# A software-pipelined attention period in another order: scores in two halves, keys multiplied by their norms one period later

## The chip, the cores and the metric

The kernel runs on one core of one Trainium2 chip. The time is the device time of one execution in microseconds (us); lower is better. Each core has five engines that run side by side, each through its own instruction stream, strictly in the order written, and that wait for each other on semaphores: PE (TensorE, the matrix engine), DVE (VectorE), ACT (ScalarE), POOL (GpSimd) and SP (SyncE, which here issues most of the transfers). Matrix products land in PSUM, eight banks of 128 x 512 float32; DVE and ACT read them there.

## The reference

The program is a stack of four layers over 4 sequences of 512 tokens and 128 features: cross attention and a feed-forward part in each. The change touches only the feed-forward part of layer 2, which is itself a six-deep local transformer. One of its layers, cut to what matters:

```python
def attn_layer(x, Wqkv, qs, ksc, Wo):            # HEADS = 16, DIM_HEAD = 64, WINDOW = 32
    q, k, v = jnp.split(x @ Wqkv, 3, -1)         # split into heads
    q = l2norm(q) * qs
    k = l2norm(k) * ksc
    q = q * cos * scale + rotate_half(q) * sin * scale
    k = k * cos * inv + rotate_half(k) * sin * inv
    out = local_attention(q, k, v)               # a window of 32 sees itself and the one before
    return out @ Wo
...
sim = jnp.einsum('bhwie,bhwje->bhwij', bq, bk2) * QK_SCALE      # QK_SCALE = 8
sim = jnp.where(mask, -jnp.finfo(sim.dtype).max, sim)
attn = jax.nn.softmax(sim, -1)
out = jnp.einsum('bhwij,bhwje->bhwie', attn, bv2)
```

A gated feed-forward layer (layer norm, `W1` with a gelu gate, `W2`) follows each attention layer. Both are added to the stream.

## The kernel before

Everything around the local transformer is left as it is. `local_transformer` works on tiles of 128 tokens: 4 tiles make a sequence (a "row" in the code), 4 sequences a layer, 6 layers, so 96 tiles. The stream of a sequence is kept transposed in `Y[b]`. The order of the work is written out by hand; no planner moves it, and each engine runs its share in just that order.

The loop is a software pipeline. In period n it works on three tiles at once: tile n (`T`) goes from `Y` to rotated, normalised queries, keys and values; tile n-1 (`T1`) from there to exponentials of its scores; tile n-2 (`T2`) from there to the residual. The feed-forward layer of a finished sequence is cut into four phases and laid into the periods by `ff_stage`, at two places in each (`second` False or True).

The stages, with the lines of the profile:

- `queries_or_keys(T, kind, c)`: half c of the queries (kind 0) or keys (kind 1). One 128 x 512 product on PE (L1842) into one of two `mm` banks, and its squares on ACT (L1844).
- `rotate`: on DVE two products with the rotary tables (L1852, L1855) and the sum of the squares (L1864); on POOL the sum of the two products (L1865).
- `normalise`: on POOL and ACT the inverse norms of all 32 heads (L1875 to L1881, ACT's logarithm and exponential among them), then four POOL products of 128 x 512 (L1884), queries first, then keys.
- `turned`: two groups of four PE transposes (L621) into two `tr` banks, and an ACT copy of each (L1896), to `qT` or `kT`; for keys, POOL also puts the last 32 columns of the tile before at the head of `kT` (L1892, or zeros, L1894).
- `values(T, x0)`: one 128 x 512 product (L1919) into a `tr` bank, an ACT copy (L1920), and small transfers issued by SP that shift the windows (L1922 to L1930).
- `scores`: on PE 8 mask products (L1940) and then 64 products of 64 x 32 by 64 x 64 (L1949), into the two banks `sc`. The profile counts a float32 product as two matmuls and two weight loads, so 128 and 128.
- `softmax`: DVE takes the largest of each row (L1959) and subtracts it (L1960), ACT takes the exponential (L1965).
- `probabilities`: eight transposes (L621, `P`) and two ACT copies (L1970). `average(T, g)`: 32 small products (L1980) into the banks `av`. `normalised(T, g)`: a reciprocal and a product on DVE (L1989, L1990) that free `av`. `attended`: eight transposes (L621, `attn`) and two ACT copies (L1999). `project_out`: 8 products (L2004). `residual`: two DVE additions into `Y` (L2011).
- The feed-forward pieces use the same two banks `sc`: `ff_moments` (L2017 and DVE's statistics), `ff_norm` (L559, DVE), `ff_turn` (L2028), `ff_gate` (L2039), `ff_up` (L2050), `ff_down` (L2062).

On PE one period before is therefore: first query product, `P` transposes, second query product, a feed-forward piece, first averages, query transposes, first key product, second averages, key transposes, second key product, `attn` transposes, all scores, output product, two value products, a feed-forward piece.

Of the kernel before, what the change touches and what calls it, by code (L numbers as in the profile page):

```python
# [21 lines left out]
F32 = mybir.dt.float32  # L22
# [4 lines left out]
ALU = mybir.AluOpType  # L27
# [3 lines left out]
NT = S // 128  # L31
# [241 lines left out]
def tile_kernel(ctx: ExitStack, tc: tile.TileContext, A: dict, out: bass.AP):  # L273
# [1530 lines left out]
    def local_transformer(Y, lf, lw, columns, tabs):  # L1804

        with ExitStack() as es:
# [21 lines left out]
            class Tile:  # L1828


                def __init__(self, i, b, tt):
                    self.i, self.b, self.tt = i, b, tt
                    self.rot, self.raw, self.ss = {}, {}, None

# [32 lines left out]

            def normalise(T):


                n = 2 * LH
                ss = T.ss.rearrange("p a b -> p (a b)")
                y = small.tile([128, n], F32, name="rn_y")
                t = small.tile([128, n], F32, name="rn_t")
                G.tensor_scalar(ss, ss, 1e-24, -0.5, ALU.max, ALU.mult)  # L1875
                SC.activation(y, ss, AF.Ln, scale=-2.0)  # L1876
                SC.activation(y, y, AF.Exp, scale=-0.5)
                G.tensor_tensor(t, y, y, ALU.mult)
                G.tensor_tensor(t, t, ss, ALU.mult)
                G.tensor_scalar(t, t, 1.5, None, ALU.add)  # L1880
                G.tensor_tensor(y, y, t, ALU.mult)  # L1881
                for (kind, c), a in sorted(T.rot.items()):
                    o = LH * kind + 8 * c
                    G.tensor_tensor(a, a, bc(y[:, o : o + 8], [128, 8, LD], 2), ALU.mult)  # L1884

            def turned(T, kind):


                lead = 32 * kind
                t = qp.tile([128, LH // 2, lead + 128], F32, name="kT" if kind else "qT")  # L1890
                if kind and T.tt:
                    G.tensor_copy(t[:, :, 0:32], T.before.kT[:, :, 128:160])  # L1892
                elif kind:
                    G.memset(t[:, :, 0:32], 0.0)  # L1894
                for c in range(2):
# [3 lines left out]
                    )  # L1899
                if kind:  # L1900
                    T.kT = t
                else:
                    T.qT = t

# [26 lines left out]

            def scores(T):

                T.banks = pair("sc").rearrange("p z (k d) -> p z k d", d=64)
                for w in range(4):
                    for z in range(2):
                        r = slice(64 * (z ^ (w // 2)), 64 * (z ^ (w // 2)) + 64)
                        PE.matmul(  # L1940
                            T.banks[32 * w : 32 * w + 32, z], identb[r, r.start : r.start + 32],
                            maskw[r, int(w + T.tt == 0)], start=True, stop=False,
                            skip_group_check=True,
                        )
                for k in range(LH // 2):
                    for w in range(4):
# [7 lines left out]

            def softmax(T):

                P = tp.tile([128, LH // 2, 2, LD], F32, name="P", bufs=1)
                mx = small.tile([128, 2, LH // 2], F32, name="la_mx")
                V.tensor_reduce(mx, T.banks, AX.X, ALU.max)  # L1959
                V.tensor_tensor(  # L1960
                    P.rearrange("p k z d -> p z k d"), T.banks,
                    bc(mx, [128, 2, LH // 2, LD], 3), ALU.subtract,
                )
                T.P = P.rearrange("p k z d -> p k (z d)")
                SC.activation(T.P, T.P, AF.Exp, scale=8.0)  # L1965
# [55 lines left out]

            def ff_norm(F):
                layernorm(F.xn, F.xn, F.found)

# [48 lines left out]

            def ff_stage(F, phase, second):
                F.w1, F.w2 = loaded[F.i][2:]
                if phase == 0 and not second:
                    ff_moments(F)
                elif phase == 1:
                    ff_gate(F, 0, 1) if second else ff_turn(F)
                elif phase == 2 and second:  # L2080
                    ff_up(F, 0, 1)
                elif phase == 2:
                    ff_gate(F, 2)
                    SC.preload_act_table_set(EXP_LN)
                elif phase == 3:
                    ff_down(F) if second else ff_up(F, 2)

            tiles = [Tile(i, b, tt) for i in range(DEPTH) for b in range(B) for tt in range(NT)]  # L2090
# [3 lines left out]
            SC.preload_act_table_set(EXP_LN)  # L2094
            for n in range(len(tiles) + 2):
                T = tiles[n] if n < len(tiles) else None
                T1 = tiles[n - 1] if 0 <= n - 1 < len(tiles) else None
                T2 = tiles[n - 2] if 0 <= n - 2 < len(tiles) else None
                m, phase = divmod(n - 6, 4)
                F = rows[m] if 0 <= m < len(rows) else None  # L2100
                if T:
# [12 lines left out]
                    T.tabs = tabs[T.i]  # L2114
                    queries_or_keys(T, 0, 0)
                if T2:
                    probabilities(T2)
                if T:
                    queries_or_keys(T, 0, 1)
                    rotate(T, 0, 0)  # L2120
                if F:
                    ff_stage(F, phase, False)
                if T2:
                    average(T2, 0)
                if T1:
                    turned(T1, 0)
                if T:
                    queries_or_keys(T, 1, 0)
                if T2:
                    normalised(T2, 0)  # L2130
                if T:
                    rotate(T, 0, 1)
                if T2:
                    average(T2, 1)
                if T1:
                    turned(T1, 1)
                if T:
                    queries_or_keys(T, 1, 1)
                if T2:
                    normalised(T2, 1)  # L2140
                if T:
                    rotate(T, 1, 0)
                if T2:
                    attended(T2)
                if T and T.tt == NT - 1 and n + 1 < len(tiles):
                    swap(tiles[n + 1].b)
                if T1:
                    scores(T1)
                if T:
                    rotate(T, 1, 1)  # L2150
                if T:
                    normalise(T)
                if T1:
                    softmax(T1)
                if T2:
                    project_out(T2)
                    residual(T2)
                if F and phase == 0:
                    ff_norm(F)
                if T:  # L2160
                    values(T, 0)
                    values(T, 1)
                if F:
                    ff_stage(F, phase, True)
            return loaded[DEPTH - 1][2:]
# [133 lines left out]
```

## Time and profile before

| | |
|---|---|
| median of 3 runs | 2462.42 us (2460.44 to 2462.8) |
| the profiled execution | 2456.04 us |
| its span in the profile | 2454.2 us |
| first to last mask product of the local transformer (L1940) | 536.7 to 2152.8 us |
| PE busy | 2228.0 us (91%) |
| DVE, POOL, ACT busy | 1759.3, 1338.6, 1298.1 us (72%, 55%, 53%) |
| mean TensorE clock granted | 0.953 of full speed |

How to read what follows. A row of the timeline has the start in us from the beginning of the span, the time in us, the engine, the line, the operation, the tile written and read, the shapes, and how many instructions of that kind follow each other. In brackets stands how long the engine was idle before the row and what ended it. "issue" means that it waited for nothing that the profile shows. PEld is the loading of weights into the matrix engine, which overlaps its products. A busy PE is not PE at its peak, because the ends of matmuls are modelled; the time from the start of one block of rows to the start of the next says more.

### The profile page before, as it was taken

Reading aid. Unit: us, or ns where it says so; the run is one execution under the profiler, and the core shown is the slowest. Engines: PE = TensorE matmul, PEld = TensorE weight load, DVE = VectorE, ACT = ScalarE, POOL = GpSimd, SP = SyncE. Lnnn points to the kernel's source line nnn. Section 1 sums busy time; section 2 is a strip of 40 time slices with the busy share of each in tenths; the row PEclk is TensorE's granted clock in tenths of the full one; section 3 lists DMA queues with packets and bytes.
Section 4 is the critical chain, followed back from the end, with each engine's and each line's share of the span. In section 5 each row is a group of like instructions: output and inputs, shape, how many; then the busy total and the mean of one; then the engine's idle time right before and its main releaser. Section 6 shows DMA issues by size and latency. Waiting matters only on the chain. (4 is left out here: it accounts for less than half of the span.)

```text
span 2454.2 us, 86703 instructions
## 1 busy us (share of the span) xinstructions
PE 2228.0 (91%) x37341; PEld 1479.5 (60%) x37341; DVE 1759.3 (72%) x3896; ACT 1298.1 (53%) x2389; POOL 1338.6 (55%) x1862
## 2 busy tenths in 40 slices
PE   7958969978999999999999999999999999989676
PEld 3536734546666666666666666666666666644355
DVE  5545356866888888777887888887878788767422
ACT  3423325645666655666666666565666666525222
POOL 2141330256667676766667766766667666710433
PEclk9868989988999999999999999999999999989688
DMA  7201110016211121111211121111211111120023
GB/s 182 68 21 41 40 60 2 1 41 135 80 35 29 35 70 36 33 29 35 75 31 36 29 79 33 29 35 27 80 31 31 35 29 35 27 67 23 26 67 95
DMA packets 134298, 116.14 MB, mean 47 GB/s; under 512 B 29506, under 2 KB 102701, under 8 KB 133917
## 3 DMA queue, kind: packets, MB, share of 16 engines
q1 hardware_dynamic: 122037, 99.67, 15.8%
q0 software_dynamic: 4608, 7.35, 0.9%
q8 instruction: 296, 4.85, 0.9%
q10 hardware_dynamic: 7271, 3.58, 0.5%
q14 instruction: 86, 0.70, 0.1%
HBM read 42.84 MB, written 21.52 MB: 26 GB/s over the span
## 5 line engine op out<-in xcount | busy, mean ns | idle before, releaser
L1865 POOL TENSOR_TENSOR rc<-rc,rs 128x512 f32<-128x512 f32 x384 | 489.8, 1276 | 400.7 <-DVE rs L1855 326.3
L1842 PE MATMUL ps_mm<-wqk,y 128*128 128x512 f32 x768 | 397.2, 599 | 5.3 <-issue 3.5
L1884 POOL TENSOR_TENSOR rc<-rc,rn_y 128x512 f32<-128x512 f32 x384 | 388.6, 1044 | 7.5
L1852 DVE TENSOR_TENSOR rc<-ps_mm,tabs 128x512 f32<-128x512 f32 x384 | 262.5, 684 | 129.8 <-ACT sq L1844 126.5
L1844 ACT ACTIVATE sq<-ps_mm 128x512 f32<-128x512 f32 x384 | 231.2, 602 | 161.4 <-PE ps_mm L1842 108.0
L1855 DVE TENSOR_TENSOR rs<-ps_mm,tabs 128x512 f32<-128x512 f32 x384 | 261.5, 681 | 0.2 <-POOL rc L1865 0.2
L1864 DVE TENSOR_REDUCE ss<-sq 128x8 f32<-128x512 f32 x384 | 259.5, 676 | 0.0
L621 PE MATMUL ps_tr<-cst,rc 128*128 128x128 f32 x1536 | 210.9, 280 | 4.3 <-POOL rc L1884 4.0
L1980 PEld LDWEIGHTS ps_av<-v,PT 64*32 64x32 f32 x12288 | 138.1, 105 | 126.5 <-PE ps_tr L621 54.1
L2004 PE MATMUL ps_av<-aT,wo 128*128 128x128 f32 x1536 | 200.7, 283 | 2.4 <-issue 2.4
L2004 PEld LDWEIGHTS ps_av<-aT,wo 128*128 128x128 f32 x1536 | 181.0, 193 | 12.6 <-issue 3.9
L621 PEld LDWEIGHTS ps_tr<-cst,rc 128*128 128x128 f32 x1536 | 165.6, 142 | 24.4 <-POOL rc L1884 5.1
L1949 PE MATMUL ps_sc<-kT,qT 64*32 64x64 f32 x12288 | 148.1, 225 | 33.6 <-issue 32.9
L1980 PE MATMUL ps_av<-v,PT 64*32 64x65 f32 x12288 | 170.3, 225 | 6.2 <-DVE attn L1990 1.7
L1949 PEld LDWEIGHTS ps_sc<-kT,qT 64*32 64x32 f32 x12288 | 141.2, 105 | 44.2 <-issue 38.1
L1056 POOL DMA_INDIRECT back<-ye,to x80 | 78.8, 985 | 147.5 <-DVE ye L1170 104.0
L1842 PEld LDWEIGHTS ps_mm<-wqk,y 128*128 128x128 f32 x768 | 124.5, 192 | 56.3 <-issue 50.1
L1965 ACT ACTIVATE P<-P 128x1024 f32<-128x1024 f32 x96 | 101.4, 1057 | 97.3 <-DVE P L1960 97.3
L1876 ACT ACTIVATE rn_y<-ss 128x32 f32<-128x32 f32 x96 | 22.0, 229 | 237.9 <-POOL ss L1875 237.9
L802 ACT ACTIVATE P<-ps,deltaT 77x512 f32<-77x512 f32 x192 | 115.8, 683 | 56.7 <-PE ps L796 53.0
L1896 ACT COPY qT<-ps_tr 128x512 f32<-128x512 f32 x192 | 103.3, 589 | 74.6 <-PE ps_tr L621 74.3
L1959 DVE TENSOR_REDUCE la_mx<-ps_sc 128x16 f32<-128x1024 f32 x96 | 116.9, 1218 | 31.0 <-PE ps_sc L1949 31.0
(399 smaller groups left out, 4368.9 us busy)
## 6 DMA issues: line engine op xcount, KB each, us to landing
v<-v SPq DMA_DIRECT2D x432, 65.0 KB
v<-v SPq DMA_DIRECT2D x96, 195.0 KB
wqk<-in_L_ffn_Wqkv_dram SPq DMA_DIRECT2D x24, 256.0 KB
sent<-xn SPq DMA_DIRECT2D x2, 2210.0 KB
xe<-sent SPq DMA_DIRECT2D x16, 260.0 KB
back<-xn SPq DMA_DIRECT2D x2, 2048.0 KB
raw<-in_L_ffn_W_dram SPq DMA_DIRECT2D x8, 512.0 KB
w<-in_L_ffn_W_dram SPq DMA_DIRECT2D x16, 256.0 KB
```

Source lines behind the costliest of these rows:

```text
L621: PE.transpose(t[:, i], src[:, i], ident)
L1842: PE.matmul(t, lhs, T.w[2 * kind + c], start=True, stop=True)
L1844: SC.activation(sq, t, AF.Square)
L1852: V.tensor_tensor(a, t, bc(T.tabs[:, 2 * kind, tt], [128, 8, LD], 1), ALU.mult)
L1855: V.tensor_tensor(r.rearrange("p h (x d) -> p h x d", x=2), t.rearrange("p h (x d) -> p h x d", x=2)[:, :, ::-1], bc(T.tabs[:, 2 * kind + ...
L1864: V.tensor_reduce(T.ss[:, kind, 8 * c : 8 * c + 8], sq, AX.X, ALU.add)
L1865: G.tensor_tensor(a, a, r, ALU.add)
L1884: G.tensor_tensor(a, a, bc(y[:, o : o + 8], [128, 8, LD], 2), ALU.mult)
L1949: PE.matmul(T.banks[32 * w : 32 * w + 32, z, k], T.qT[r, k, 32 * w : 32 * w + 32], T.kT[r, k, 32 * w : 32 * w + 64], start=False, stop=Tru ...
L1959: V.tensor_reduce(mx, T.banks, AX.X, ALU.max)
L1980: PE.matmul(T.means[32 * w : 32 * w + 32, x0, k], T.PT[r, 4 * g + k, 32 * w : 32 * w + 32], (T.v1 if w % 2 else T.v2)[r, x0, 4 * g + k], s ...
L2004: PE.matmul(t, T.wo[:, c], T.aT[:, c], start=(c == 0), stop=(c == 7))
```

## The change

The loop body becomes a table, `period`, of stages, each with how many tiles it lags, and is run through in order. The new order on PE is: a value product, second query product, `P` transposes, a feed-forward piece (`ff_second`, one period later than before), first averages, first query product, query transposes, a feed-forward piece (`ff_first`), first key product, second averages, key transposes, mask and first half of the scores (k 0 to 3), second key product, `attn` transposes, second half of the scores, the other value product, output product.

`normalise` is cut in two: `inverse_norms` and the products of the queries stay in the tile's own period, at its end; the products of the keys come in the next period, early on POOL. `residual` moves to the start of the next period (lag 3), `ff_norm` right behind it. `kT` is allocated, and its head copied, one period earlier (`keys_before`). `softmax` is cut into `largest` and `exponentials` with one value product between them. The loop runs one period longer. The arithmetic, the shapes and the numbers of instructions are the same.

```diff
-            def normalise(T):
+            def inverse_norms(T):
...
                 G.tensor_tensor(y, y, t, ALU.mult)
-                for (kind, c), a in sorted(T.rot.items()):
-                    o = LH * kind + 8 * c
-                    G.tensor_tensor(a, a, bc(y[:, o : o + 8], [128, 8, LD], 2), ALU.mult)
+                T.inv = y
+
+            def normalise(T, kind):
+                for c in range(2):
+                    a, o = T.rot[kind, c], LH * kind + 8 * c
+                    G.tensor_tensor(a, a, bc(T.inv[:, o : o + 8], [128, 8, LD], 2), ALU.mult)
...
+            def keys_before(T):
+
+                T.kT = qp.tile([128, LH // 2, 160], F32, name="kT")
+                if T.tt:
+                    G.tensor_copy(T.kT[:, :, 0:32], T.before.kT[:, :, 128:160])
                 else:
-                    T.qT = t
+                    G.memset(T.kT[:, :, 0:32], 0.0)
...
-            def scores(T):
+            def scores(T, g):
...
-                for k in range(LH // 2):
+                for k in range(4 * g, 4 * g + 4):
...
-            def ff_stage(F, phase, second):
...
+            def ff_first(F, phase):
+                if phase == 0:
                     ff_moments(F)
                 elif phase == 1:
-                    ff_gate(F, 0, 1) if second else ff_turn(F)
-                elif phase == 2 and second:
-                    ff_up(F, 0, 1)
+                    ff_turn(F)
                 elif phase == 2:
                     ff_gate(F, 2)
                     SC.preload_act_table_set(EXP_LN)
+                else:
+                    ff_up(F, 2)
+
+            def ff_second(F, phase):
+                if phase == 1:
+                    ff_gate(F, 0, 1)
+                elif phase == 2:
+                    ff_up(F, 0, 1)
                 elif phase == 3:
-                    ff_down(F) if second else ff_up(F, 2)
+                    ff_down(F)
+
+            period = (
+                (values, 0, 0),
+                (residual, 3),
+                (queries_or_keys, 0, 0, 1),
+                (ff_norm, 1),
+                (probabilities, 2),
+                (normalise, 1, 1),
+                (rotate, 0, 0, 1),
+                (ff_second, 1),
+                (average, 2, 0),
+                (queries_or_keys, 0, 0, 0),
+                (turned, 1, 0),
+                (normalised, 2, 0),
+                (rotate, 0, 0, 0),
+                (ff_first, 0),
+                (queries_or_keys, 0, 1, 0),
+                (average, 2, 1),
+                (turned, 1, 1),
+                (keys_before, 0),
+                (normalised, 2, 1),
+                (scores, 1, 0),
+                (queries_or_keys, 0, 1, 1),
+                (rotate, 0, 1, 0),
+                (attended, 2),
+                (scores, 1, 1),
+                (rotate, 0, 1, 1),
+                (inverse_norms, 0),
+                (largest, 1),
+                (values, 0, 1),
+                (exponentials, 1),
+                (project_out, 2),
+                (normalise, 0, 0),
+            )
...
-            for n in range(len(tiles) + 2):
+            for n in range(len(tiles) + 3):
...
+                for stage, lag, *which in period:
+                    if stage in by_row:
+                        m, phase = divmod(n - lag - 6, 4)
+                        if 0 <= m < len(rows) - 1:
+                            F = rows[m]
+                            F.w1, F.w2 = loaded[F.i][2:]
+                            stage(F, phase)
+                    elif 0 <= n - lag < len(tiles):
+                        stage(tiles[n - lag], *which)
```

## The prediction

> **What bounds the kernel now.** I read the page's shares first, then the table of stretches (PE 486 of 500 us busy from 1200 to 1700, DVE 406, POOL 345, ACT 303), then PE's waits, then two periods of the timeline. The change lives between the first and the last mask product, 536.69 to 2152.83 us: 95 periods, mean 17.01 us.
>
> ```profile
> PE 2228.0 (91%) x37341; PEld 1479.5 (60%) x37341; DVE 1759.3 (72%) x3896; ACT 1298.1 (53%) x2389; POOL 1338.6 (55%) x1862
> ...
> q8 instruction: 296, 4.85, 0.9%
> ```
>
> ```profile
> PE ps_sc L1949 <- issue: 22.6, 23, 1.5
> PE ps_tr L621 <- ACT v L1920: 3.4, 12, 0.3
> PE ps_sc L2028 <- DVE xn L559: 2.8, 7, 0.5
> ```
>
> These are PE's waits from 700 to 2000 us: total, times, longest. The engine almost never waits for another one; what it waits for most is "issue", inside the scores. Two periods of the timeline show both kinds:
>
> ```profile
> 1205.88 1.02 PE L1842 MATMUL ps_mm<-wqk,y 128*128 128x512 f32 x2
> ...
> 1206.93 0.60 ACT L1844 ACTIVATE sq<-ps_mm 128x512 f32<-128x512 f32 x1 [1.73 <-PE ps_mm L1842]
> ...
> 1207.57 0.69 DVE L1852 TENSOR_TENSOR rc<-ps_mm,tabs 128x512 f32<-128x512 f32 x1
> ...
> 1212.89 1.09 PE L621 MATMUL ps_tr<-cst,rc 128*128 128x128 f32 x8
> ...
> 1213.58 1.08 ACT L1896 COPY kT<-ps_tr 128x512 f32<-128x512 f32 x2 [0.73 <-PE ps_tr L621]
> ...
> 1213.82 1.02 PE L1842 MATMUL ps_mm<-wqk,y 128*128 128x512 f32 x2
> ...
> 1214.68 1.04 PE L621 MATMUL ps_tr<-cst,attn 128*128 128x128 f32 x8
> ...
> 1215.64 0.41 PE L1940 MATMUL ps_sc<-maskw,identb 64*32 64x512 bf16 x8
> ...
> 1215.87 1.46 PE L1949 MATMUL ps_sc<-kT,qT 64*32 64x64 f32 x128
> ...
> 1217.26 2.05 PE L2004 MATMUL ps_av<-aT,wo 128*128 128x128 f32 x16
> 1217.45 1.22 DVE L1959 TENSOR_REDUCE la_mx<-ps_sc 128x16 f32<-128x1024 f32 x1
> ...
> 1218.70 1.23 DVE L1960 TENSOR_TENSOR P<-ps_sc,la_mx 128x1024 f32<-128x1024 f32 x1
> ...
> 1219.96 1.06 ACT L1965 ACTIVATE P<-P 128x1024 f32<-128x1024 f32 x1 [0.67 <-DVE P L1960]
> ...
> 1233.22 1.27 PE L1949 MATMUL ps_sc<-kT,qT 64*32 64x64 f32 x107
> ...
> 1235.69 0.42 PE L1949 MATMUL ps_sc<-kT,qT 64*32 64x64 f32 x21 [1.20 <-issue]
> ```
>
> PE goes from block to block without a gap; the scores take 1.39 us from start to start (1215.87 to 1217.26), but 2.82 in the second period. Of the 96 score blocks 30 are drawn out, 36.5 us in all without one early outlier: 0.38 us a period. Undisturbed, the four periods of a feed-forward row take 17.35, 15.42, 16.71 and 16.71, mean 16.55. So a period is PE's own work plus 0.46, nearly all of it "issue".
>
> What "issue" is: PE's two rows have 75,789 records, and queue 8 moves 296 packets of 16,384 bytes, so 256 records to a packet. Counted in order, each of the stalls in L1949 past 620 us begins at record 193 of a block of 256. A packet of that queue starts 0.7 to 1.5 us before such a stall, and PE resumes 2.3 to 2.7 us after the packet's start (once 3.1): at 1233.10 and 1235.69 here. The dense scores eat a block of instructions faster than the next arrives.
>
> The page "Runtime: NRT & Kernel Launch" of the Trainium skill, section "Instruction fetch mechanics", has the blocks of 256 and calls the cost of crossing one "mostly hidden". The trace disagrees here: 30 stalls of a median 1.26 us. By the page's rule both orders would be free of them, there would be no credit for instructions, and the change would come to +43 instead of the +31 worked out below.
>
> **The change part by part** (96 periods; us).
>
> *Splitting the scores.* PE pays for going between whole-array and small products: the last transpose before the mask takes 0.202 instead of 0.109, so 0.093 in; the last score takes 0.146 where scores follow each other every 0.010, so 0.136 out. One more run of small products costs 0.23: **+22**.
>
> *The first half behind the key transposes.* Before, the second key product and the `attn` transposes (0.86 + 0.97) lay between them and covered ACT's copy. Now only the mask does. PE is ready at 0.93 + 0.09 + 0.22 = 1.24 after the transposes begin; the first copy ends at 0.69 (1212.89 to 1213.58) + 0.59 = 1.28, and PE follows a copy by about 0.10 (1214.16 to 1214.25): 1.38. Wait 0.14, **+14**, from 0 to 0.25. Queued behind it on PE is the second key product, which everything next waits for.
>
> *From the second key product to the `P` transposes.* That chain is: product to DVE's first rotation 1.69 (1205.88 to 1207.57), three rotation steps 1.80 (starts are 0.60 apart), 1.25 to the subtraction, 1.26 to the exponential, 1.06 for it, 0.07 to PE: 7.13. PE's work between: 0.86 + 0.97 + 0.76 (half the scores) + 0.86 + 1.89 + 0.86 + 0.86 = 7.06. Wait 0.07, and 0.04 more because the second `tr` bank waits for a value copy behind the exponential: **+10**, from 0 to 25.
>
> *The period without `ff_second`*, one in four. `P` transposes are followed at once by averages that need ACT's copies: behind the exponential ACT has a value copy 0.47, squares 0.49, copy 0.58. Taking 0.10 off for the exponential's overlap and 0.10 on to PE gives 1.54; PE is there after 0.11 + 0.87 + 0.09. Wait 0.47. In the same period `ff_norm` takes 3.78 of DVE (1239.18 to the next row at 1242.96) ahead of a rotation:
>
> ```profile
> 1239.18 3.75 DVE L559 TENSOR_SCALAR xn<-xn,ln_mv,ln_rs 128x128 f32<-128x128 f32 x4
> ...
> 1242.96 0.69 DVE L1852 TENSOR_TENSOR rc<-ps_mm,tabs 128x512 f32<-128x512 f32 x1
> ```
>
> From the end of the subtraction: residual 0.6, `ff_norm` 3.78, rotation 1.79, reciprocal 0.21, product 0.69, 0.1 to PE: 7.2, where PE wants its second averages at 6.7. About 0.47 each over 24 such periods would be 22; one wait shifts the next, and I take **+14**, from 0 to 22.
>
> *Waits that go.* `ff_norm` has a period more before `ff_turn`: its block of four transposes takes a mean 0.92, the like block of L2017 0.53: 23 x 0.39 = 9. The `P` transposes' waits for value copies, 0.05 a period, 5. Second averages in the `ff_moments` period, about 0.2 x 23 = 5. Together **-19**, from 0.
>
> *Moved at no cost.* POOL's key products in the next period are needed at the key transposes, some 6 us later; the query products end about 1.4 before their transposes. POOL has 31% idle. Without that cover each 0.5 late is 48. SP's value transfers go earlier or stay, and are read two periods on. The head of `kT` is copied a period ahead.
>
> *The start.* The first instruction on PE is now a value product whose two 256 KB loads are issued at 515.1, 1.3 before PE's first product at 516.36; at the 222 to 298 GB/s of that stretch they take about 2: **+2**.
>
> *Instructions.* At best all 36 go. But a packet whose block ends in the scores after their first 45 records or so starts just behind the start of the key transposes (1213.04 against 1212.89) and has 3.0 to 3.3 us until PE needs it; it needs 2.3 to 2.9. The new order takes 1.83 out of those 3.15 and puts 0.14 back: 1.5 remain, a stall of about 0.9 where none was. Some 83 of 256 positions are hit: 96 x 83/256 x 0.9 = 28. Blocks ending late in the second half: their packet can't start until PE's stream has passed the wait for the copy at 1.4, about 0.9 behind it as in the rows above, so lands at 4.75 where PE runs that half from 4.0 to 4.7: 0.3 x 78/256 x 96 = 9. That is as much as is saved. Between -36 and 0 I take **-12**, nearer to the row at 1213.04.
>
> Sum: 22 + 14 + 10 + 14 - 19 + 2 - 12 = **+31**. The profiled execution of 2456.04 would become 2487; the median shown is 6.4 above it, so 2462.4 + 31 = **2493**.
>
> **Rivals.**
> - *The stalls vanish altogether.* The two halves have 20 records in 1.83 us between them, so no block is eaten in one go. For: they sat in nothing but dense scores. Against: the 1.5 us above. The last term is -36: 2462.4 + 7 = **2469**.
> - *Not slower: instructions come in time and so does the exponential.* One mechanism, at the second key product: if PE's margins there (0.14 and 0.07, a few hundredths from zero) are met, only the switches stay of what is added every period. 22 - 36 - 19 + 2 + 7 (half the fourth-period waits) = -24: **2438**. It decides once the added waits are below about 0.2 a period. Against: both chains are fixed durations, read from rows that repeat.
> - *The norms become the bound.* Queries are multiplied last on POOL; if that lies 1.4 + 0.5 late, PE's query transposes wait in each period: 2493 + 48 = **2541**. For: Newton steps and squares sit on POOL and ACT in turn. Against: POOL's idle share.
>
> **How the numbers follow.** Forecast 0.55, stalls vanish 0.20, not slower 0.15, norms 0.10. What can't be told from no change is 0.2%, 4.9 us. Slower: 0.55 + 0.20 x 0.6 + 0.10 = 0.77; same: 0.20 x 0.25 + 0.15 x 0.1 = 0.07; faster 0.16. The forecast's own range, by the bounds of its waits, is 2473 to 2516. The range for 8 in 10 cuts the tails of the last two rivals: **2448 to 2525**.
>
> **What would show it.** A mean period between masks of 17.3 (now 17.01). The first half's first product following the key transposes by 1.4, with ACT's `kT` copy as releaser; "issue" still among PE's waits, now within the first half; `P` transposes waiting for the exponential by 0.1; in one period of four, averages waiting for ACT's `PT` and DVE's `attn`. Wrong, if "issue" is gone from L1949's successor, if the first half doesn't wait, or if POOL's L1884 ends PE's idle time.

## The result, and the profile after

| | before | changed |
|---|---|---|
| median | 2462.61 us of 4 runs (2460.44 to 2466.53) | 2495.4 us of 4 runs (2492.77 to 2501.42) |
| ratio | | 1.0134, 95% interval 1.0118 to 1.0149 |
| the profiled execution, its span | 2456.04, 2454.2 us | 2501.42, 2499.6 us |
| from mask to mask, mean of 95 periods | 17.01 us | 17.33 us (546.09 to 2192.91) |
| from the start of PE's last block ahead of the local transformer to its first local product | 6.92 us | 9.27 us |

The change costs 33 us. Of these 95 x 0.32 = 31 lie in the periods and about 2 at the start. The other 12 us between the two spans lie outside the local transformer, where runs of one kernel differ as much (last section).

The page of the changed kernel, its shares and the instruction queue:

```profile
PE 2291.4 (92%) x37341; PEld 1485.2 (59%) x37341; DVE 1768.2 (71%) x3896; ACT 1285.1 (51%) x2389; POOL 1338.4 (54%) x1862
...
q8 instruction: 295, 4.83, 0.8%
```

The instructions are as many, and PE is 63 us busier with them. PE's waits of the changed kernel from 700 to 2000 us (total, times, longest) are the answer to the table of before:

```profile
PE ps_sc L1954 <- issue: 8.0, 10, 1.6
PE ps_av L1986 <- ACT PT L1976: 5.7, 18, 0.3
```

"issue" has fallen from 22.6 to 8.0. So PE waits less than before and is still later: what was added is not in a table of waits. It shows when one period of the timeline is read from start to start (start, time, engine, line, operation, in brackets the idle time before and what ended it):

```profile
1239.58 1.09 PE L621 MATMUL ps_tr<-cst,rc 128*128 128x128 f32 x8
1240.60 0.41 PE L1944 MATMUL ps_sc<-maskw,identb 64*32 64x512 bf16 x8
1240.91 0.86 PE L1954 MATMUL ps_sc<-kT,qT 64*32 64x64 f32 x64
1241.69 1.12 PE L1842 MATMUL ps_mm<-wqk,y 128*128 128x512 f32 x2
1242.66 1.04 PE L621 MATMUL ps_tr<-cst,attn 128*128 128x128 f32 x8
1243.62 0.86 PE L1954 MATMUL ps_sc<-kT,qT 64*32 64x64 f32 x64
1244.41 1.12 PE L1923 MATMUL ps_tr<-wv,yw 128*128 128x512 f32 x2
```

Read downwards. The transposes last 1.02 (0.93 where a product follows them), the mask 0.31 (0.23 before), the halves 0.78 and 0.79 (together 1.57, in one piece 1.39), and the key product between them 0.97 where it took 0.86. No row has a bracket, so none of this counts as idle time of PE: every block is a little longer. One of the four is a wait all the same. The modelled end of the mask hides it on PE, but the weight load of the first half shows it, and so does ACT's copy in the same period:

```profile
1240.90 0.70 PEld L1954 LDWEIGHTS ps_sc<-kT,qT 64*32 64x32 f32 x64 [0.20 <-ACT kT L1895]
```

```profile
1240.27 1.07 ACT L1895 COPY kT<-ps_tr 128x512 f32<-128x512 f32 x2 [0.73 <-PE ps_tr L621]
```

The first of the two copies ends about 1240.85, and the scores start at 1240.91. In every period past 700 us the first score starts 0.05 us after a copy to `kT` ends.

The account by kind of block makes the same reading for a whole run: mean time in a period (72 periods past 700 us) from the start of a block to the start of the next. Two profiled runs of each kernel are given; e1, the changed kernel without the split, and e7, the split alone, are experiments told below.

| us a period | before | changed | e1 | e7 |
|---|---|---|---|---|
| mask | 0.23, 0.23 | 0.37, 0.37 | 0.23, 0.23 | 0.31 |
| scores | 1.76, 1.72 | 1.73, 1.71 | 1.75, 1.68 | 1.80 |
| query and key products | 3.66, 3.65 | 3.83, 3.83 | 3.64, 3.65 | 3.86 |
| query and key transposes | 1.86, 1.86 | 1.90, 1.90 | 1.80, 1.80 | 1.95 |
| `P` transposes | 0.89, 0.89 | 1.08, 1.08 | 0.99, 0.99 | 0.90 |
| averages | 1.65, 1.65 | 1.62, 1.62 | 1.62, 1.62 | 1.67 |
| value products | 1.72, 1.72 | 1.83, 1.82 | 1.87, 1.85 | 1.72 |
| output product | 1.93, 1.93 | 1.80, 1.78 | 1.85, 1.80 | 1.89 |
| feed-forward | 2.35, 2.34 | 2.22, 2.22 | 2.22, 2.22 | 2.34 |
| `attn` transposes | 0.97, 0.97 | 0.97, 0.97 | 0.97, 0.97 | 0.97 |
| period | 17.00, 16.96 | 17.34, 17.30 | 16.94, 16.81 | 17.40 |

### The profile page after: what moved, and what is told of

Same layout as the page of the kernel before. It is cut to its first block, busy times and chain, and to the rows that moved or that the text cites. A ratio compares the mean times of both kernels' runs of the same rounds, so it can differ in the third digit from the quotient of the medians.

```text
span 2499.6 us, 86702 instructions
## 1 busy us (share of the span) xinstructions
PE 2291.4 (92%) x37341; PEld 1485.2 (59%) x37341; DVE 1768.2 (71%) x3896; ACT 1285.1 (51%) x2389; POOL 1338.4 (54%) x1862
## 4 chain that ended last, share of the span: by engine, by line
PE 68%; issue 11%; DVE 10%; ACT 6%; DMA 3%; POOL 2%; SPq 1%; another core or an unknown queue 0%; ACTq 0%; POOLq 0%; DVEq 0%
PE ps_mm L1842 13%; PE ps_tr L621 12%; PE ps_av L1986 6%; PE ps_tr L1923 5%; PE ps_av L2010 5%; PE ps_sc L1954 5%; PE ps_sc L2046 2%; PE ps_sc L2057 2%; PE ps_sc L2069 2%; ACT sq L1844 2%; PE ps L812 1%; PE ps L821 1%; DVE P L1966 1%; DVE la_mx L1962 1%; PE ps L1717 1%
## 5 line engine op out<-in xcount | busy, mean ns | idle before, releaser
L1842 PE MATMUL ps_mm<-wqk,y 128*128 128x512 f32 x768 | 414.5, 622 | 2.2 <-DVE rs L1855 1.8
L2010 PEld LDWEIGHTS ps_av<-aT,wo 128*128 128x128 f32 x1536 | 187.6, 193 | 45.6 <-issue 45.5
L621 PEld LDWEIGHTS ps_tr<-cst,rc 128*128 128x128 f32 x1536 | 173.3, 142 | 65.6 <-issue 42.0
L621 PE MATMUL ps_tr<-cst,rc 128*128 128x128 f32 x1536 | 205.9, 277 | 4.0 <-POOL rc L1887 4.0
L2010 PE MATMUL ps_av<-aT,wo 128*128 128x128 f32 x1536 | 188.1, 276 | 0.0
L1954 PE MATMUL ps_sc<-kT,qT 64*32 64x64 f32 x12288 | 167.8, 224 | 15.1 <-issue 11.3
L1954 PEld LDWEIGHTS ps_sc<-kT,qT 64*32 64x32 f32 x12288 | 134.8, 105 | 54.3 <-issue 29.6
L1996 DVE TENSOR_TENSOR attn<-ps_av,la_den 128x512 f32<-128x512 f32 x192 | 132.8, 691 | 6.6
L1895 ACT COPY kT<-ps_tr 128x512 f32<-128x512 f32 x192 | 103.2, 590 | 55.4 <-PE ps_tr L621 55.4
L621 PEld LDWEIGHTS ps_tr<-cst,P 128*128 128x128 f32 x768 | 82.1, 141 | 80.3 <-ACT P L1971 72.5
```

Source lines behind the costliest of these rows:

```text
L621: PE.transpose(t[:, i], src[:, i], ident)
L1842: PE.matmul(t, lhs, T.w[2 * kind + c], start=True, stop=True)
L1954: PE.matmul(T.banks[32 * w : 32 * w + 32, z, k], T.qT[r, k, 32 * w : 32 * w + 32], T.kT[r, k, 32 * w : 32 * w + 64], start=False, stop=Tru ...
L1996: V.tensor_tensor(T.attn[:, 4 * g : 4 * g + 4].rearrange("p k x d -> p x k d"), T.means[:, :, :, 0:LD], bc(den, [128, 2, 4, LD], 3), ALU.mult,
L2010: PE.matmul(t, T.wo[:, c], T.aT[:, c], start=(c == 0), stop=(c == 7))
```

## The experiments

A time is compared with that of the kernel before in runs on the same chip, as a ratio: the kernel before took 2470.23, 2409.56, 2455.06 and 2411.46 us on the chips of the four groups of runs (e1 to e4; a2, e5 to e7; b3, e8; e9, e10). Where an expectation names a time for the wrong one of these, its difference is compared.

**e1: the two halves together again** (against the changed kernel)

```diff
-                (scores, 1, 0),
                 (queries_or_keys, 0, 1, 1),
                 (rotate, 0, 1, 0),
                 (attended, 2),
+                (scores, 1, 0),
                 (scores, 1, 1),
```

> The changed kernel with the two halves of the scores side by side again, both behind the second key product and the transposes of attn; all else as changed. Theory A (the split costs the time, by switches and the wait for the kT copy, and gives some back in instruction fetch): the switches and the slower 128x512 products go (-0.41 x 96 = -39), the mask's wait for the copy of kT goes (0.142 x 96 = -14), the fetch stalls come back (+22): about 2464, between 2452 and 2478, with the idle time of the scores put down to issue back at about 30 us. Theory B (the split is free; the late multiplication of the keys, the sums by phase or other moved steps cost the time): 2490 or more.

Measured: 2455.42 us, ratio to before 0.9928 (0.9902 to 0.9955). PE's waits of e1 from 700 to 2000 us:

```profile
PE ps_sc L1954 <- issue: 23.0, 16, 3.4
PE ps_av L1986 <- ACT PT L1976: 5.5, 19, 0.3
```

One step put back, and the kernel is 0.7% faster than before instead of 1.3% slower. That is theory A, with a larger step than its -31 and than its bound of -43 (ratio difference 0.020, 49 us; by the periods 0.45 x 96 = 43). "issue" is back at 23.0. The split is the whole loss, and the rest of the change is a gain that the split hid.

**e2: the key product ahead of the first half**

```diff
+                (queries_or_keys, 0, 1, 1),
                 (scores, 1, 0),
-                (queries_or_keys, 0, 1, 1),
                 (rotate, 0, 1, 0),
```

> The changed kernel with the second key product ahead of the first half of the scores; the split stays, around the transposes of attn alone. Theory A: the wait of the mask for the kT copy goes (-14), the second key product stands behind transposes instead of behind scores and takes 0.86 us instead of 0.96 (-10 in all), most of the switches stay: about 2472, between 2464 and 2482. Theory B (the split and its place are free): 2490 to 2500.

Measured: 2462.56 us, ratio 0.9963 (0.9948 to 0.9978), period 17.00. By the ratios that is 42 us less than the changed kernel, where theory A had 23 and at most 31. The waits of e2, same stretch:

```profile
PE ps_av L1986 <- DVE attn L1996: 5.6, 14, 0.4
PE ps_sc L1954 <- issue: 4.2, 7, 1.2
```

The mask is back at 0.23 in every period, so its wait was for the `kT` copy. The split remains, around the `attn` transposes alone, and "issue" falls to 4.2: with 0.97 us of large work between the halves and a covered copy, nearly all fetch stalls go. Against e1, undisturbed, this split adds 0.17 in the halves, 0.06 in the `attn` transposes and 0.09 in the key product, 0.32, and the scores' excess over 1.39 falls by 0.25 to 0.31 (5.7 us in 92 blocks, e1 and its repeat 34.5 and 28.3 in 92 and 90): roughly even. A wait for `attn` in one period of four costs 0.1 a period on top, and by the ratios e2 is 0.3% slower than e1. So a split need not be dear; this one was dear by its place. One part of theory A fell: the key product stays at 0.95 behind transposes, because now small products follow it. The price sits on both sides of a block, and moving a neighbour doesn't save it.

**e3: the split alone, in the kernel before**

```diff
...
+                if T1:
+                    scores(T1, 0)
                 if T:
                     queries_or_keys(T, 1, 1)
...
-                    scores(T1)
+                    scores(T1, 1)
```

> The kernel before with one edit: the scores in two halves, the first right behind the transposes of the keys, the second where the scores were, so around the second key product and the transposes of attn; no other step is moved. Theory A: +39 for switches and slower products, +14 for the wait for the kT copy, -22 for fewer fetch stalls: about 2493, between 2483 and 2505; the idle time of the scores put down to issue falls from 33 us to about a third. Theory B (the split is free): 2458 to 2468.

Measured: 2533.2 us, ratio 1.0247 (1.0221 to 1.0273): +61 us, twice theory A. The waits of e3, same stretch:

```profile
PE ps_sc L1950 <- POOL kT L1892: 29.7, 51, 1.6
PE ps_tr L621 <- ACT v L1920: 7.3, 19, 0.4
PE ps_sc L1950 <- issue: 2.5, 8, 0.5
```

A releaser that neither theory had: POOL's copy of the last 32 keys to the head of `kT`. In the kernel before it stands behind two rotations on POOL and has the key product and the `attn` transposes as cover; with the scores drawn forward it has none, and the mask takes 0.82 instead of 0.23. The change issues that copy a period earlier (`keys_before`), so this cost is one that it avoided.

**e7: e3 with that copy a period earlier**

```diff
...
+                if T:
+                    keys_before(T)
                 if T1:
                     scores(T1, 0)
...
```

> e3 (the kernel before with the scores split alone) with one more edit, taken from the change: the 32 keys of the tile before are copied to the head of kT by GpSimd in the period before, not in the period of the scores. Theory: e3's mask waited 0.81 us a period for that copy, which stood behind two rotations on GpSimd's queue; with it early the mask waits only for ScalarE's copy, 0.37: -0.44 x 95 = -42 us, 2491, between 2484 and 2500. Then the split alone costs about 21 us (switches and waits +50, fetch stalls -28). Rival (the copy is not what the mask waited for): 2525 to 2535.

Measured: 2443.12 us, ratio 1.0144 (1.012 to 1.0169), +34 us; against e3 that is -25, where -42 was expected. The waits of e7, same stretch:

```profile
PE ps_sc L1952 <- issue: 12.9, 16, 1.1
PE ps_tr L621 <- ACT v L1922: 7.3, 19, 0.4
```

POOL's wait is gone and the mask is down by 0.51 a period, but the period only by 0.33: "issue" rises from 2.5 to 12.9. The reading that fits both: while PE waited for POOL, the next block of instructions was arriving; without that wait it must be waited for by itself. Two waits at one place overlap, and taking one away gives less than its row says. The split alone costs 17.40 - 16.98 = 0.42 a period, and e1 says what the rest of the change is worth: 16.87 - 16.98 = -0.11. Their sum, 0.31, is close to the changed kernel's 17.32 - 16.98 = 0.34 (means of the runs in the table).

**e4: the keys multiplied in their own period** (against the changed kernel)

```diff
-                (normalise, 1, 1),
...
                 (normalise, 0, 0),
+                (normalise, 0, 1),
```

> The changed kernel with the keys multiplied by their norms at the end of their own period, behind the queries, instead of in the next one. Theory A (the late keys cost and save nothing: GpSimd does the same work in nearly the same order, and its end is not what the key transposes wait for): 2490 to 2500. Theory C (the late keys hold up the key transposes or the copies of kT, and so part of the loss): 2465 to 2485.

**a2: the changed kernel on another chip**

> The changed kernel itself, on the chip of these runs, as the mark for e1, e2 and e4. The accounts of the periods give 39 us between it and the unsplit kernel (2455): about 2494 to 2497, and then the late keys (e4, 2493) cost nothing. If it is 2500 or more (2470 x 1.0134 = 2503), the late keys or something outside the periods hold some 8 us that the accounts do not show.

Measured: e4 1.0093 (1.0068 to 1.0118), a2 1.0124 (1.0096 to 1.0152). The periods are 17.31 and 17.30, and none of their blocks differs by more than 0.01. In the periods the late keys cost and save nothing. The intervals of the two ratios overlap; a2's ratio would be 2501 us on e4's chip, the second case of its expectation. e4's lies below that of the first comparison too, by 0.4%, and whether some us are gained outside the periods stays open.

**e5: a feed-forward piece later, in the kernel before**

```diff
-                if F:
-                    ff_stage(F, phase, False)
                 if T2:
                     average(T2, 0)
                 if T1:
                     turned(T1, 0)
+                if F:
+                    ff_stage(F, phase, False)
```

> The kernel before with one edit: the first part of the feed-forward's stage is issued behind the transposes of the queries instead of ahead of the first averages. Theory: this is where the changed kernel got its gain outside the split; ff_turn's wait for the end of ff_norm (0.47 in one period of 4) goes, 24 x 0.37 = 9 us, and the switches stay as many: 2461, between 2456 and 2466. Rival: the gain was from another move (the values apart, the residual in the next period): 2468 to 2474.

Measured: 2499.62 us, ratio 1.0379 (1.0348 to 1.0409): +90 us where -9 was expected. The DVE rows of e5 in a period with `ff_moments`, and the PE row that waits for them:

```profile
1244.97 0.87 DVE L547 BATCH_NORM_STATS2 ln_st<-xn 128x6 f32<-128x128 f32 x4 [2.14 <-ACT xn L2019]
1245.76 0.36 DVE L549 BATCH_NORM_AGGREGATE ln_mv<-ln_st 128x2 f32<-128x6 f32 x4
1246.04 0.18 DVE L1989 RECIPROCAL la_den<-ps_av 128x8 f32<-128x8 f32 x1
1246.25 0.69 DVE L1990 TENSOR_TENSOR attn<-ps_av,la_den 128x512 f32<-128x512 f32 x1
```

```profile
1247.09 0.85 PE L1980 MATMUL ps_av<-v,PT 64*32 64x65 f32 x64 [2.01 <-DVE attn L1990]
```

The first averages were done at about 1242.7, but `normalised` is queued on DVE behind the statistics, and these wait 2.14 us for a piece that PE now does later. The averages' only bank pair stays taken. The same happens in the period in which `ff_up`'s DVE work comes ahead of `normalised` (key product to second averages 1.94 us for 0.95); the two make up nearly all of PE's 55.7 us of waiting for `attn` between 700 and 2000 us. The first averages, now right behind the second query product, wait another 11.1 for `PT`. The piece has the same place on PE in the changed kernel, but there `normalised` is issued ahead of it. So this edit doesn't test where the gain came from; it shows that the place on PE and the place on DVE must move together.

**e6: first averages behind the query product** (against e1)

```diff
-                (average, 2, 0),
                 (queries_or_keys, 0, 0, 0),
+                (average, 2, 0),
```

> The unsplit kernel e1 with the first averages behind the first query product instead of ahead of it. Theory: in the period without ff_second the averages wait 0.47 us for the copies of PT; a product of 0.86 between covers it, 0.126 x 96 = 12 us in all: 2443, between 2437 and 2449. Rival: the wait comes back elsewhere (attn 0.86 us later at its transposes, or the products' place taken from the rotation): 2450 to 2462.

Measured: 2393.08 us, ratio 0.9931 (0.9911 to 0.9951), the same as e1; period 16.93. The waits of e6, 700 to 2000 us:

```profile
PE ps_sc L1954 <- issue: 24.1, 18, 3.2
PE ps_av L1986 <- DVE attn L1996: 6.7, 19, 0.4
```

The wait for `PT` is gone and one for `attn` has come, 19 times as before: the rival. Rows of such a period in e6:

```profile
1211.39 3.63 DVE L559 TENSOR_SCALAR xn<-xn,ln_mv,ln_rs 128x128 f32<-128x128 f32 x4
...
1217.09 0.69 DVE L1996 TENSOR_TENSOR attn<-ps_av,la_den 128x512 f32<-128x512 f32 x1
```

```profile
1217.93 0.85 PE L1986 MATMUL ps_av<-v,PT 64*32 64x65 f32 x64 [0.40 <-DVE attn L1996]
```

Between these two rows DVE has no gap: `ff_norm` puts it 3.6 us behind, and the second averages find it there.

**e9: `ff_norm` on ACT** (against e6; the shift is made on POOL)

```diff
-                    layernorm(F.xn, F.xn, F.found)
+                    mv, rs = F.found
+                    shift = small.tile([128, NT], F32, name="ln_sh")
+                    G.tensor_tensor(shift, mv[:, :, 0], rs, ALU.mult)
+                    G.tensor_scalar(shift, shift, -1.0, None, ALU.mult)
+                    for t in range(NT):
+                        SC.activation(
+                            F.xn[:, t], F.xn[:, t], AF.Identity,
+                            scale=rs[:, t : t + 1], bias=shift[:, t : t + 1],
+                        )
...
-                (ff_norm, 1),
...
                 (largest, 1),
+                (ff_norm, 0),
```

> e6 with ff_norm's four subtract-and-scale instructions taken from VectorE (3.63 us in one period of 4, 1211.39 in e6's trace) and done by ScalarE as a scaled copy with a shift, one period earlier behind la_mx, where ScalarE waits for the scores. Theory: in the period without ff_second VectorE is 3.6 us behind because of ff_norm, and that is what the second averages (0.50), the turn and the key transposes (0.06 each) wait for in e6, and the PT copies' wait in e1 is the same lateness of the period in another place: -0.62 x 24 = -15 us on e6, a ratio to before of 0.987, between 0.983 and 0.990. Rival (the wait is for the averages' own results and not for VectorE's queue): 0.992 to 0.995.

Measured: 2464.56 us, ratio 1.0236 (1.0204 to 1.0268), outside the theory's range and the rival's. A wait of PE and a group of ACT (busy, mean ns; then idle before and its releaser) in e9:

```profile
PE ps_tr L621 <- ACT P L1971: 48.8, 18, 3.2
```

```profile
L2035 ACT ACTIVATE xn<-xn,ln_sh,ln_rs 128x128 f32<-128x128 f32 x72 | 29.6, 482 | 33.9 <-POOL ln_sh L2033 33.9
```

The wait that the theory named is gone: in that period the first key product, which in e6 took 1.44 with the wait behind it, takes 0.95. That doesn't prove the theory, because in the same period PE itself now waits 2.7 us for `P` at its transposes, and so much lateness alone would cover 0.5. The two small POOL instructions for the shift stand behind POOL's rotations and inverse norms, ACT waits 1.9 us for them each time, and the exponential is queued behind on ACT. The work was moved to an engine with idle time, but behind another one's queue.

**e8: the second averages straight ahead of the scores** (against e6)

```diff
-                (average, 2, 1),
                 (turned, 1, 1),
                 (keys_before, 0),
-                (normalised, 2, 1),
                 (queries_or_keys, 0, 1, 1),
                 (rotate, 0, 1, 0),
-                (attended, 2),
+                (average, 2, 1),
+                (normalised, 2, 1),
                 (scores, 1, 0),
                 (scores, 1, 1),
+                (attended, 2),
```

> e6 with the second averages moved behind the second key product, straight ahead of the mask and the scores, and the transposes of attn behind the scores: two blocks of small products become one, the reverse of the change's split. Theory A (each block of small products that stands alone costs about 0.38 us: 0.19 at its end, 0.09 and 0.10 in the work before and behind it; a longer block waits more for instructions): -0.38 and the wait for attn (-0.12) a period, +0 to +0.33 of fetch stalls: about -0.3 x 96 = -29 us on e6, a ratio to before of 0.981, between 0.975 and 0.986. Rival (the blocks' ends are not what the split paid for, or the fetch stalls and the later copies of aT take it all back): 0.990 or more.

Measured: 2539.2 us, ratio 1.0334 (1.0296 to 1.0372), period (output product to output product) 17.84 against e6's 16.92. The block's start, its end and what follows in e8:

```profile
1215.37 0.42 PE L1944 MATMUL ps_sc<-maskw,identb 64*32 64x512 bf16 x5
1215.52 1.47 PE L1954 MATMUL ps_sc<-kT,qT 64*32 64x64 f32 x128
1216.92 0.66 PE L621 MATMUL ps_tr<-cst,attn 128*128 128x128 f32 x4
1220.66 1.01 PE L621 MATMUL ps_tr<-cst,attn 128*128 128x128 f32 x4 [3.08 <-issue]
```

and two of its waits from 700 to 2000 us:

```profile
PE ps_sc L1954 <- issue: 55.2, 37, 3.0
PE ps_tr L1923 <- ACT aT L2005: 14.8, 59, 0.9
```

The result is the rival's: what theory A saves is taken back more than whole. Both halves of theory A's working show. The ends are saved: the second averages follow one another and go over into the mask after 0.58 and not 0.79, the first key product falls from 0.95 to 0.86, the transposes behind it from 0.93 to 0.87. But 200 small matmuls in a row (64, 8 and 128) more than double the stalls: "issue" goes from 24.1 to 55.2, and the transposes of `attn` come so late that a value product waits for the copy to `aT`. From start to start the scores take 0.52 a period more than in e6 and the `attn` transposes 0.48. The bound put on the stalls, 0.33 a period, was too small, and the wait for the copy had no term.

**b3: the kernel before once more; e10: e1 once more**

> The kernel before itself, profiled again, to see how far its mean period between masks (17.00 us) and its idle time put down to issue (33 us) vary from run to run. If the fetch stalls vary, the period should be between 16.9 and 17.2, and the rest of the blocks the same to 0.01; the difference of e1 against it (-0.06 a period, -6 us, where the times say -18) is then to be read against a period of up to 17.1.

> e1 again beside e9. The times of e1 gave 0.9928 [0.9902, 0.9955], the periods only 0.02 to 0.06 us less than before (-2 to -6 us, 0.998). If the periods tell it all, 0.996 to 1.000; if the gain is real and lies where the two traces differ by chip, 0.991 to 0.995.

Measured: b3 2453.3 us with a period of 16.96; e10 2392.68 us, ratio 0.9937 (0.991 to 0.9964), period 16.81. The kernel before varies by 0.05 a period and e1 by 0.13, more than half of it in the fetch stalls of the scores (excess over 1.39, all blocks past 600 us: before 40.9 and 34.6 us, e1 34.5 and 28.3). The means of two runs each differ by 0.11 x 96 = 10 us, the ratios say 15 to 18. e10's ratio lies in the range that stood for a real gain. That e1 and e6 are faster than both kernels is measured three times; some 6 us of the gain aren't located.

## Why the prediction was right

The time was forecast as 2493 and is 2495.4: +33 for +31. The mechanism was the forecast's, and of its steps only one wait of two in the period without `ff_second` stays out. But three terms were off by 5 to 15 us, in both directions; that the sum came out within 2 us is in part luck. Measured terms are differences of blocks (e1 against changed, before against e1) x 96, or x 24 for the period that comes once in four.

| step | predicted | measured |
|---|---|---|
| splitting the scores | +22 | +37: 0.093 in the transposes ahead, 0.187 in the halves, 0.101 in the product behind |
| first half behind the key transposes | +14 | +14: mask 0.369 for 0.226 |
| second key product to the `P` transposes | +10 | +15: 0.07 in the query product ahead, 0.09 in the transposes |
| period without `ff_second` | +14 | +16: `P` transposes 1.33 for 0.87 in e1, first averages 0.14, first key product 0.05 |
| waits that go | -19 | -23: `ff_turn` 0.93 to 0.44, of which 0.40 was a wait; query product and `P` transposes 0.35; second averages in the `ff_moments` period 0.22 |
| start | +2 | +2: 9.27 us for 6.92 to the first local product |
| instructions | -12 | -25: the scores' excess 40.9 and 34.6 us before, 14.4 and 11.2 changed |
| sum | +31 | +36 by the terms; +33 by the times |

*The switches were mis-sized.* The step took the last transpose (0.093) and the last score (0.136) from the rows and stopped there. It left out the work behind the block: any 128 x 512 product right behind small products takes 0.962 and not 0.861. The rows of before had this, if read one by one: behind the scores the first matmul of the output product takes 0.213 and the others 0.112, and behind the averages the first transpose takes 0.165 and the others 0.109. But a block was costed by its own last row and the one ahead of it. The Trainium skill states a possible cause in "TensorEngine Tiling (Array Packing)", section "Key Properties": changing the tiling mode drains the engine. The runs agree in that a block cut in two is 0.187 longer, and e8 in that two blocks joined are shorter; no run here tells a drain from another cause, and the page has no price.

*The wait for `kT` is shown, its size is partly luck.* PE follows the copy by 0.05 and not by 0.10 (the row at 1214.25 that this was read from is a weight load 0.43 behind PE's own product at 1213.82). So in three periods of four the mask takes 0.31, a wait of 0.08 and not 0.14. In the fourth, with two `ff_gate` pieces, it takes 0.56: there ACT's copies stand behind a gelu and a table load of 1.28 us, for which the step had no term. The mean of the four is the forecast's 0.14.

*The chain to the `P` transposes* ends as forecast at the exponential: in the changed kernel the transposes mostly start 0.05 us after its end, in e1 0.53 (medians). The wait is 0.07 and the second bank's 0.04, as worked out; the other 0.05 is the first transpose (0.165 for 0.109), which the step left out.

*Instructions were mis-sized the other way.* The credit was bounded by -36 and 0 and taken at -12; it is -25. Most of the stalls that the step feared in the new places didn't come (13 over 0.3 us remain of 30). "issue" is still there, within the first half and the second. All over 0.5 us that remain begin at the same place of a block of 256 records as before, but for one that is a record off. e8 bears out that dense small products are the cause: more of them in a row stall more. e8 also goes against "mostly hidden" (the page "Runtime: NRT & Kernel Launch", section "Instruction fetch mechanics") once more: 55 us in 1300. (In the kernel before PE resumes 2.2 to 2.7 us after a packet's start, once 3.1; the 2.3 of the prediction was a little high.)

*One wait of two came.* In the period without `ff_second` the averages wait for `PT`, 0.47 as worked out. The second averages' wait for `attn` was costed as separate; in the trace the first wait delays PE enough to cover it, as "one wait shifts the next" allowed; no wait of PE for `attn` is left in the changed kernel's list. e6 shows that it stands ready: take the first away, and the second is there, 0.48.

Of the signs named, the period (17.33 for 17.3), the wait for `kT` (transposes to first score 1.33 for 1.4, in the mean 1.39), "issue" in the first half, `P` transposes late by 0.1 and averages waiting for `PT` were all there; averages waiting for `attn` were not.

The rivals: the stalls don't vanish altogether; e2 shows what it would take (a large piece between the halves, no copy to wait for), and then the split is about even. *Not slower* asked for both margins at the second key product to be met; they were missed by 0.14 and 0.16. With both met the measured terms would have left 37 + 2 + 8 - 23 - 25 = -1 (8 is half the fourth-period waits): no gain, because the switches cost more than that rival gave them. *The norms become the bound* didn't come: no product of POOL, of queries or of keys, ends idle time of PE in the changed kernel between 700 and 2000 us.

## What to carry over

A block of small products costs at both ends and in its neighbours: price it by the start-to-start times of the blocks around it, once with and once without it next to them, and not by its own last row. Cutting a dense block gave back in instruction fetch about what its ends cost in the best case here (e2), with a large piece between the halves and nothing of the first half still being copied; elsewhere it lost. e1, which leaves the block whole and keeps the rest of the change, is 0.6% to 0.7% faster than the kernel before. When a step moves on one engine, move its successors in the other engines' queues with it (e5), and look at what stands ahead in each queue that it now depends on (e9). Expect a wait that shares its place with another to give back less than its row (e7, e6).

## What the runs showed that was not expected

- *Waits seem to hide fetch stalls.* e3 with 29.7 us of waiting for POOL has 2.5 us of "issue", e7 without it 12.9.
- *Fetch latency is steady, its effect is not.* In e1, e2 and e8 PE resumes 2.2 to 2.9 us after the start of the packet that it waits for, and the stall is what PE couldn't fill of that. The same kernel's stalls differ by 6 us from run to run.
- *Chips differ outside the loop.* The kernel before takes 2409.6 to 2470.2 us by chip, the periods hardly differ. These are stretches of the changed kernel's two profiled runs, first on the chip of the first comparison, then on a2's (stretch, length, busy time of PE, PEld, DVE, ACT and POOL, granted clock, DMA share, GB/s):

```profile
0.00:520.00 520.00, 434.64 (x3721) 268.07 (x3721) 294.56 (x1040) 207.18 (x394) 136.02 (x194) 0.89 0.19 49
700.00:2000.00 1300.00, 1281.85 (x24790) 842.17 (x24789) 1048.75 (x1822) 771.42 (x1429) 874.84 (x1231) 1.00 0.15 40
```

```profile
0.00:490.00 490.00, 411.18 (x3717) 258.33 (x3722) 294.36 (x1041) 206.83 (x394) 135.61 (x194) 0.93 0.20 52
700.00:2000.00 1300.00, 1283.00 (x24871) 842.81 (x24869) 1051.43 (x1827) 768.61 (x1426) 873.10 (x1231) 1.00 0.15 40
```

Some 3720 matmuls lie in the first 520 us at a granted clock of 0.89, and as many in the first 490 at 0.93, while the periods run at 1.00 on both. A time of this kernel is therefore only worth something beside the kernel before on the same chip.
